# Shifting attention rows to ScalarE, doubling the last block's side steps and spreading the reload of the node features in a two-layer graph network kernel

## The chip, the core and the metric

The kernel runs on one core of one Trainium2 chip. The metric is the device time of one execution in microseconds (us), as the median of several runs. TensorE is called PE, VectorE DVE, ScalarE ACT, GpSimd POOL and SyncE SP, as in the profile. PE multiplies, DVE and ACT work elementwise, POOL issues the indirect transfers (gathers and scatters of rows), and SP issues the plain transfers.

## What is computed

There are 1250 nodes with 512 features and 40000 edges, sorted by destination. The first layer is graph attention with 8 heads, followed by a dense network; the second layer adds up edge messages and ends in two dense layers with batch norm. Cut to what matters here:

```python
# layer 0, h = layer_norm(x)
xl = (h @ Wl).reshape(-1, HEADS, C); xr = (h @ Wr).reshape(-1, HEADS, C)
e = einsum('ehc,hc->eh', leaky_relu(xl[src] + xr[dst], 0.2), att)
ex = exp(e - segment_max(e, dst)[dst])
alpha = ex / (segment_sum(ex, dst)[dst] + 1e-16)
x1 = x + segment_sum(alpha[..., None] * xl[src], dst) + gat_bias
x2 = x1 + gelu(layer_norm(x1) @ W1 + b1) @ W2 + b2
x = layer_norm(x + x2)
# layer 1
msg = relu(x[src] + edge_attr @ W_e + b_e)
h = (1 + eps) * x + segment_sum(msg, dst)
h = silu(bn(h @ W1 + b1)); h = silu(bn(h @ W2 + b2))
return layer_norm(x + h)
```

## The kernel before, in words

Nodes are sorted by their number of incoming edges and cut into ten blocks of 128 (block 9 has 98); the table `KB` says how many edges the largest node of each block has (44 in block 0, 25 in block 9). A "row" of a block is one edge of each of its 128 nodes, one per partition, so a row is a gather of 128 table lines.

**The attention part** (`attention`) goes through the blocks from 9 to 0. A block is cut into groups of at most 20 rows and a group into chunks of at most 5 rows; there are 22 groups and 77 chunks. Block 0 has three groups of 20, 16 and 8 rows, with 4, 4 and 2 chunks; they are called A, B and C here, and their chunks A0 to A3, B0 to B3, C0 and C1. In the loop over chunks, `scores` gathers a chunk's rows into `xg` (7 buffers, POOL) and reduces them on DVE to one score per edge and head. At the last chunk of a group follow `softmax` (DVE) and `exp` (ACT). `weigh` is a generator that runs one group behind: while the chunks of one group are scored, those of the group before are multiplied by their softmax weights `w`. In each of its chunks the first `na` rows are multiplied on ACT, with 8 instructions per row (one per head), and the rest in a single DVE instruction; then PE adds all rows up into `sums`. After a group, `leave` copies `sums` out (ACT, `ab`) and folds them on PE (`pacc`), and `merge` adds them to the block's `acc` on DVE.

Beside this the dense part of finished blocks is done in small steps, written as generators:

- `head_of` takes a finished `acc` through transposes and a layer norm to `hT`; its steps lie between `yield`s and are made by `step_others`, which is called once a chunk, after `scores`, `softmax` and `merge` and before `weigh`. A step that yields "late" is continued at the end of the chunk by `step_lates`.
- `body_of` is the two-layer dense network of a block, as 19 parts (16 products of W1, the gelu one part later, the W2 product three parts later). A call of `part` makes one of them; `weigh` calls it under a quota of 3 a chunk, or 4 when a block stands in `ready`. Only one body is under way at a time (`held["py"]`).
- `end_of` adds the residual, normalizes, writes the block to `xo_t` and scatters it to `xb_t`. `step_pres` makes a step of it at the start of a chunk.

The instructions of PE, ACT, DVE and POOL in this part are kept in the order in which the program makes them. After the last chunk the last group is weighed, and a loop finishes the bodies of blocks 1 and 0.

**The edge part** (`second`) starts when all blocks stand in `xb_t`. For each pair of rows two gathers fetch `xs` (12 buffers of two rows), PE makes the edge product `pe`, and DVE adds and accumulates relu (L1871, L1872); every fourth full pair is added on PE and put through relu on ACT (L1867, L1868), and DVE only accumulates it (L1876). Blocks go in the order 9, 0, 1, ..., 8. When a block is complete, `finish` adds the block's own features from `x_out` (L1834) and transposes the result; the first dense layer then runs between later pairs. `x_out` holds all ten blocks; it is loaded from `xo_t` by ten transfers of 256 KB issued by SP at the second pair (`i == 1`), after that pair's add (L1877 to L1880). It is read by `finish` and at the very end.

Then come the two dense layers' normalizations, the second dense layer and the output scatter.

Of the kernel before, what the change touches and what calls it, by code (L numbers as in the profile page):

```python
# [713 lines left out]
ORDER = range(NB - 1, -1, -1)  # L714
# [3 lines left out]
def parts(k, most):  # L718

    n = -(-k // most)  # L720
    cut = [k * i // n for i in range(n + 1)]
    return [(a, b - a) for a, b in zip(cut, cut[1:])]
# [3 lines left out]
def gnn_kernel(ctx, tc, x, src, dst, edge_attr, ln1_g, ln1_b, Wl, Wr, att, gat_bias,  # L726
# [515 lines left out]
    BLOCKS = (NB - 1, *range(NB - 1))  # L1242
# [3 lines left out]
    def attention(s1, xb_t, xo_t, eb_t, back, lone, follow):  # L1246
# [243 lines left out]
        def step(t):  # L1490
            got = next(t, 0)
            if got == 0:
                others.remove(t)
            elif got == "late":
                lates.append(t)

        def step_pres():

            todo = list(pres)
            pres.clear()  # L1500
            for t in todo:
                step(t)
# [25 lines left out]
        def some(n):  # L1528
            for _ in range(min(n, quota[0])):
                quota[0] -= 1  # L1530
                part()
# [56 lines left out]
        def weigh(g):  # L1588

            w, n = g["w"], g["n"]  # L1590
            g["gd"] = gd = sp.tile([P, HEADS], F32, name="gd")
            V.tensor_reduce(gd, w[:, :n, :].rearrange("p n h -> p h n"), axis=AX.X, op=OP.add)
            g["at"], g["rows"] = [0, 0], [sum((cn + 1 - i) // 2 for _, cn in g["cuts"]) for i in range(2)]
            for c, (c0, cn) in enumerate(g["cuts"]):
                na = 1 if g is groups[-1] else (cn + c % 2) // 2
                rest = leave()
                xv = g["xg"][c][:, na:cn, :].rearrange("p n (h c) -> p n h c", c=CX)[:, :, :, 1:]
                V.tensor_mul(xv, xv, w[:, c0 + na:c0 + cn, :, None].to_broadcast([P, cn - na, HEADS, CH]))
                for j in range(c0, c0 + na):
                    xv = row_of(g, j)  # L1600
                    for h in range(HEADS):
                        A.activation(xv[:, h, :], xv[:, h, :], AF.Copy, scale=w[:, j, h:h + 1])
                    some(1)
                    next(rest, 0)
                some(quota[0])
                for _ in rest:
                    pass
                if not c:
                    g["sums"] = [aq.tile([P, D], F32, name=f"sums{k}") for k in range(2)]
                for j in range(cn):  # L1610
                    add_up(g, c0 + j // 2 if j % 2 else c0 + cn - 1 - j // 2, j % 2)
                yield
            weighed.append(g)
# [62 lines left out]
        groups, weighed, folded = [], [], []  # L1676
        for b in ORDER:
            cuts = {0: [(0, 20), (20, 16), (36, 8)], 1: [(0, 16), (16, 16), (32, 8)]}.get(b) or parts(KB[b], GN)
            for k0, n in cuts:
                groups.append(dict(b=b, k0=k0, n=n, first=(k0 == 0), last=(k0 + n == KB[b]), cuts=parts(n, CN), xg=[]))  # L1680
        groups[0]["cuts"] = [(0, 2)] + [(2 + a, k) for a, k in parts(groups[0]["n"] - 2, CN)]
        blk = dict(b=ORDER[0], nxr=nxr9)
        ahead = weighing = None
        piece = [0]
        for i, g in enumerate(groups):
            if g["first"]:
                if i:
                    blk, ahead = ahead, None
                blk["m"] = low
                if g["b"] == 0:  # L1690
                    drain("acc", 2)
                    held["acc"] += 1
                    blk.update(over)
                    blk["acc"] = bp.tile([P, D], F32, name="acc", bufs=3)
                    nc.sync.dma_start(blk["acc"], oa_t)
            g["blk"] = blk
            g["S"] = sp.tile([P, GN + 1, HEADS], F32, name="S", bufs=2)
            nc_ = len(g["cuts"])
            left = len(groups[i - 1]["cuts"]) if i else 0
            for c in range(nc_):  # L1700
                step_pres()
                scores(g, c)
                if c == nc_ - 1:
                    softmax(g)
                if c == 0:
                    if not i:
                        others.append(wr_order())
                    if g["first"] and g["b"] != ORDER[-1]:
                        others.append(slots_of(g["b"] - 1))
                    if g is groups[-1] and held["xx"] < 3:  # L1710
                        rows_of(blk)
                    weighing = weigh(groups[i - 1]) if i else None
                if folded:
                    merge(folded.pop())
                if c == 1 and g["first"] and g["b"] != ORDER[-1]:
                    ahead = normed_of(g["b"] - 1)
                if c == 2 and g["first"] and ahead:
                    others.append(xr_of(ahead))
                if i > 3 and piece[0] < len(pieces):
                    piece_of(piece[0])  # L1720
                    piece[0] += 1
                step_others()
                quota[0] = 4 if ready else 3
                todo = -(-left // (nc_ - c))
                left -= todo
                for _ in range(todo):
                    next(weighing)
                if left == 0 and weighing:
                    next(weighing, 0)
                if not todo:  # L1730
                    for _ in leave():
                        some(1)
                if c == nc_ - 1:
                    exp(g)
                some(quota[0])
                step_lates()
# [34 lines left out]
    def second(s2, early, xb_t, xo_t, eb_t, eps1, back, V, A, T):  # L1771
# [25 lines left out]
        with ExitStack() as s3:  # L1797
# [48 lines left out]
            for i, (n, j, m) in enumerate(pairs):  # L1846
                b, c0, cn = pieces[n]
                if j == 0:
                    if c0 == 0:
                        pd = hq.tile([P, 2, D], F32, name="pd")  # L1850
                        if b == 0:
                            nc.tensor.matmul(pd[:, 0, :], back, h9, start=True, stop=True)
                            nc.vector.memset(pd[:, 1, :], 0.0)
                        else:
                            (nc.vector if n else V).memset(pd, 0.0)
                    if n + 1 < len(pieces):
                        eaTs[n + 1] = turn(n + 1, nc.scalar if n else A)
                at = KO[b] + c0 + j
                xs = xp_.tile([P, 2, D], F32, name="xs")
                for k in range(m):  # L1860
                    gather(xs[:, k, :], xb_t, src_i[:, at + k:at + k + 1])
                if i + 1 < len(pairs):
                    product(i + 1)
                pe, xv, pv = pes.pop(i), xs[:, :m, :], pd[:, :m, :]
                if by_pe(i):
                    for k in range(m):
                        nc.tensor.matmul(pe[:, k, :], ident, xs[:, k, :], start=False, stop=True)  # L1867
                    nc.scalar.activation(xv, pe, AF.Relu)  # L1868
                    late.append((xv, pv))
                else:  # L1870
                    add = nc.vector.tensor_add(xv, xv, pe[:, :m, :])  # L1871
                    nc.vector.scalar_tensor_tensor(pv, xv, 0.0, pv, op0=OP.max, op1=OP.add)  # L1872
                last = c0 + j + m == KB[b]
                if late and (last or not by_pe(i)):
                    xv, pv = late.pop()
                    nc.vector.tensor_add(pv, xv, pv)  # L1876
                if i == 1:  # L1877
                    for k in BLOCKS:
                        after(nc.sync.dma_start(x_out[:, k, :], xo_t[k * P:(k + 1) * P, :]), [add],
                              "behind the first gathers")  # L1880
                if j % 4 or j + m == cn or b > 6:
                    if work is None and todo:
                        work = first_dense(todo.pop(0))
                    if work is not None and next(work, 0) == 0:
                        work = None
                if last:
                    if b == NB - 1:
                        h9 = ep.tile([P, D], F32, name="h9", bufs=1)
                        nc.vector.tensor_copy(h9, pd[:, 0, :])
                        nc.vector.tensor_add(h9, h9, pd[:, 1, :])  # L1890
                    finish(b, pd)
                    todo += ready.get(b, [])
# [125 lines left out]
```

## Time and profile before

| what | value |
|---|---|
| median of 5 runs | 1594.36 us (1588.75 to 1604.56) |
| the profiled execution | 1604.1 us, with a span of 1602.3 us |
| mean granted TensorE clock | 0.871 |
| busy share of the span | PE 76%, DVE 72%, POOL 54%, ACT 45% |
| first to last start of an attention row sum (`sums`) | 124.5 to 858.2 us |
| first to last start of an edge gather (`xs`) | 921.3 to 1455.2 us |
| issue of the ten `x_out` loads | 930.5 to 937.0 us |
| start of the last output scatter | 1597.1 us |

The page lists busy time by engine and line; the view of stretches gives each engine's busy time between two moments, the view of waits says who waited for whom, and the timeline lists one engine's work in order, with the idle time before an item and what ended it in square brackets. Inside the attention part nearly all instructions have the line of one helper (L782), so they are told apart by the tiles that they write and read.

### The profile page before, as it was taken

What the parts mean: (1) busy time and instruction counts of PE and PEld (TensorE: products, weight loads), DVE (VectorE), ACT (ScalarE), POOL (GpSimd) and SP (SyncE); (2) the same over time, 40 slices, a digit from 0 to 9 for tenths busy, and PEclk for the clock granted to TensorE, in tenths of its full rate; (3) what the DMA queues carried; (4) which work ended last, traced back from release to release, by engine and by line L of the source; (5) the groups of instructions that cost most, each with busy time, mean ns of one, the idle gap of its engine ahead of it and who ended that gap; (6) DMA issues with size and microseconds to landing.
All of it is one profiled execution on the core that took longest, in us unless ns stands there. A gap on an engine that the chain in (4) does not pass through costs nothing. (4 is left out here: it accounts for less than half of the span.)

```text
span 1602.3 us, 16505 instructions
## 1 busy us (share of the span) xinstructions
PE 1214.3 (76%) x5204; PEld 572.1 (36%) x5204; DVE 1145.8 (72%) x1472; ACT 716.0 (45%) x2063; POOL 864.0 (54%) x789
## 2 busy tenths in 40 slices
PE   5846669799897969796978945575675988698793
PEld 4431225344353424242534512121221443243552
DVE  6859898888889896979982135676676777668233
ACT  3526467676776757768676201110110221121433
POOL 2368777665767776757530075656465555642002
PEclk8977779999997989898979967888797998899896
DMA  6257966545666665546424185666565565652001
GB/s 204 95 150 217 345 172 174 158 137 163 185 185 181 182 187 158 153 111 167 124 83 139 34 284 159 203 188 190 160 204 171 178 179 180 180 147 75 0 0 67
DMA packets 89152, 251.16 MB, mean 157 GB/s; under 512 B 17214, under 2 KB 19268, under 8 KB 88543
## 3 DMA queue, kind: packets, MB, share of 16 engines
q0 software_dynamic: 61008, 199.11, 43.7%
q1 hardware_dynamic: 28047, 50.91, 9.0%
q8 instruction: 43, 0.70, 0.2%
q14 instruction: 54, 0.44, 0.1%
HBM read 225.86 MB, written 24.22 MB: 156 GB/s over the span
## 5 line engine op out<-in xcount | busy, mean ns | idle before, releaser
L782 POOL DMA_INDIRECT xg<-xl_t,src_i x333 | 422.7, 1269 | 207.6 <-issue 116.7
L749 POOL DMA_INDIRECT xs<-xb_t,src_i x333 | 315.7, 948 | 222.1 <-DVE pd L1872 102.5
L1826 PE MATMUL pe<-we,eaT 64*128 64x512 f32 x666 | 227.3, 742 | 145.5 <-issue 72.4
L782 ACT ACTIVATE xg<-xg,w 128x64 f32<-128x64 f32 x1328 | 331.0, 345 | 0.1
L782 PE MATMUL sums<-xg,ident 64*64 64x512 f32 x1332 | 217.3, 728 | 106.0 <-DVE xg L782 83.6
L1871 DVE TENSOR_TENSOR xs<-xs,pe 128x1024 f32<-128x1024 f32 (+1 forms) x130 | 153.6, 1188 | 124.6 <-remote 77.0
L782 DVE TENSOR_TENSOR z<-xg,nxr 128x1440 f32<-128x1440 f32 (+4 forms) x154 | 197.6, 1324 | 39.6 <-DMA xg<-xl_t,src_i 34.5
L782 DVE TENSOR_REDUCE S<-z 128x32 f32<-128x2080 f32 (+2 forms) x77 | 192.2, 2496 | 2.6
L782 PEld LDWEIGHTS pu<-hT,w 128*128 128x128 f32 x1280 | 163.7, 196 | 69.6 <-issue 61.7
L782 PE MATMUL py<-w,uT 128*128 128x512 f32 x320 | 164.9, 607 | 14.9 <-ACT uT L782 11.5
L782 PE MATMUL pu<-hT,w 128*128 128x128 f32 x1280 | 172.3, 282 | 0.7 <-issue 0.7
L1872 DVE SCALAR_TENSOR_TENSOR pd<-xs,pd 128x1024 f32<-128x1024 f32 (+1 forms) x130 | 155.7, 1197 | 3.3
L1826 PEld LDWEIGHTS pe<-we,eaT 64*128 64x128 f32 x666 | 65.4, 215 | 251.1 <-issue 145.7
L782 PEld LDWEIGHTS sums<-xg,ident 64*64 64x64 f32 x1332 | 60.8, 155 | 252.2 <-issue 117.1
L1868 ACT ACTIVATE xs<-pe 128x1024 f32<-128x1024 f32 x40 | 41.0, 1025 | 220.8 <-PE pe L1867 101.2
L782 DVE TENSOR_TENSOR xg<-xg,w 128x1024 f32<-128x1024 f32 (+2 forms) x77 | 100.1, 1305 | 0.0
L782 ACT ACT_TABLE_LOAD x71 | 91.1, 1283 | 7.3 <-DVE sh L782 4.3
L782 PE MATMUL pacc<-ab,fold 128*64 128x512 f32 x88 | 57.9, 746 | 45.5 <-ACT ab L782 42.8
L1867 PE MATMUL pe<-xs,ident 128*128 128x512 f32 x160 | 89.4, 670 | 0.0
L741 POOL DMA_INDIRECT out_dram<-z,v_i x10 | 10.0, 1004 | 131.9 <-ACT z L782 129.5
L782 DVE TENSOR_TENSOR z<-z,sgn 128x768 f32<-128x768 f32 (+2 forms) x77 | 78.2, 1016 | 0.0
L782 PE MATMUL pz<-z,v 128*128 128x512 f32 (+1 forms) x192 | 71.0, 529 | 6.2 <-ACT z L782 6.2
(264 smaller groups left out, 1298.2 us busy)
## 6 DMA issues: line engine op xcount, KB each, us to landing
eb_t<-fe SPq DMA_DIRECT2D x38, 256.0 KB
ea<-eb_t SPq DMA_DIRECT2D x38, 256.0 KB
w<-in_L_gnn_W_dram SPq DMA_DIRECT2D x8, 1024.0 KB
xg<-xl_t,src_i POOLq DMA_INDIRECT x333
xs<-xb_t,src_i POOLq DMA_INDIRECT x333
v<-in_L_gnn_W_dram SPq DMA_DIRECT2D x2, 2048.0 KB
xo_t<-xo SPq DMA_DIRECT2D x10, 256.0 KB
x_out<-xo_t SPq DMA_DIRECT2D x10, 256.0 KB
```

Of the source, the lines that this page charges most:

```text
L741: s = nc.gpsimd.indirect_dma_start(out=table, out_offset=bass.IndirectOffsetOnAxis(ap=idx, axis=0), in_=rows, in_offset=None, bounds_check ...
L749: return nc.gpsimd.indirect_dma_start(out=rows, out_offset=None, in_=table, in_offset=bass.IndirectOffsetOnAxis(ap=idx, axis=0))
L782: ins = getattr(engine, name)(*args, **kw)
L1826: nc.tensor.matmul(pe[:, k, :], eaTs[n][r, j // 2, :], we[r, :], start=True, stop=not by_pe(i))
L1867: nc.tensor.matmul(pe[:, k, :], ident, xs[:, k, :], start=False, stop=True)
L1868: nc.scalar.activation(xv, pe, AF.Relu)
L1871: add = nc.vector.tensor_add(xv, xv, pe[:, :m, :])
L1872: nc.vector.scalar_tensor_tensor(pv, xv, 0.0, pv, op0=OP.max, op1=OP.add)
```

## The change

Three edits:

1. `weigh`: the number of rows that ACT multiplies in a chunk of `cn` rows goes from half of `cn` (rounded down in chunks with an even index, up in odd ones) to half rounded up in even ones and half of `cn + 2`, rounded down, in odd ones. Before, the last group (C) alone had one such row per chunk; now the last two (B and C) have.
2. In the chunks of block 0, `step_others` is called once more, right after `step_pres` and ahead of `scores`.
3. Only the `x_out` loads of blocks 9 and 0 are issued at the second pair. Each following block's load is issued at the second pair of the block before it in the order.

```diff
@@ weigh
-                na = 1 if g is groups[-1] else (cn + c % 2) // 2
+                na = 1 if g in last else (cn + 1 + c % 2) // 2
@@ attention, after the list of groups
+        last = groups[-2:]
@@ attention, loop over chunks
                 step_pres()
+                if g["b"] == ORDER[-1]:
+                    step_others()
                 scores(g, c)
@@ second, loop over pairs
-                if i == 1:
-                    for k in BLOCKS:
+                if c0 == 0 and j == 2:
+                    for k in BLOCKS[:2] if i == 1 else BLOCKS[BLOCKS.index(b) + 1:BLOCKS.index(b) + 2]:
                         after(nc.sync.dma_start(x_out[:, k, :], xo_t[k * P:(k + 1) * P, :]), [add],
                               "behind the first gathers")
```

## The prediction

> **What bounds the kernel now.** I read the view of stretches first, then the waits of the attention part, then the timelines of the two places that the edits touch. The middle of the attention part, the end of it, and the edge part's first 50 us, as stretches (busy us and count of PE, PEld, DVE, ACT, POOL; granted clock, DMA share, GB/s):
>
> ```profile
> 120.00:823.00 703.00, 560.42 (x2856) 264.65 (x2858) 611.32 (x672) 483.18 (x1634) 486.72 (x391) 0.89 0.61 175
> 820.00:860.00 40.00, 33.08 (x195) 14.85 (x188) 24.71 (x37) 30.05 (x101) 3.02 (x2) 0.91 0.09 30
> 860.00:884.00 24.00, 22.55 (x117) 14.66 (x118) 4.67 (x10) 12.49 (x25) 0.00 (x0) 1.00 0.65 221
> 921.00:976.00 55.00, 21.33 (x51) 6.49 (x47) 18.11 (x16) 2.89 (x4) 37.07 (x39) 0.62 0.79 248
> ```
>
> In the first, DVE is busy 87%, PE 80%, ACT 69%: DVE leads, but no engine is alone. After 820 DVE is no longer it; PE and ACT share the end of the attention, and from 860 to 884 PE works nearly without a gap. From 921 to 976 DVE and PE stand idle for two thirds of the time while the DMA engines are at 79%. What DVE waited for in 120 to 823 (total, times, longest):
>
> ```profile
> DVE z L782 <- DMA xg<-xl_t,src_i: 24.9, 10, 5.6
> DVE t L782 <- PE pm L782: 11.1, 2, 5.9
> DVE t L782 <- PE pacc L782: 10.2, 5, 4.6
> DVE gd L782 <- ACT w L782: 7.8, 2, 4.9
> ```
>
> All its waits come to 83 us. Gathers make up some 25; behind most of the others stands ACT, directly or through PE (`pacc` needs ACT's copy of `sums`, `w` is ACT's exp).
>
> **Edit 1 in the middle (groups before B).** Counting the cuts with both formulas, the two leave 29 rows more on ACT (group B has 4 fewer). DVE's price of a row is a difference of forms: 1748 ns for three rows, 1215 for two, 0.53 us. ACT's: a run of 8 instructions takes 2.02 us (merged, at 339.68). So DVE gives up 29 x 0.53 = 15.5 us and ACT takes on 29 x 2.02 = 58.6 us. Neither is all on the path. The bounds are -15.5 us (ACT's rows wholly in its idle time) and +58.6 us (wholly on the path). ACT sits idle for 703 - 483 = 220 us there, mostly waiting for PE's transposes in chunks with a head or a query projection; in those chunks a further row is cover. In chunks with a body it has little: from 724.7 to 748 it runs without a gap and `sums` at 745.93 starts as ACT's rows end. Queued behind a longer ACT run are the exp (its reader `gd` usually has 7 us of scoring before it), the square root of the norms (same) and the copies of `sums`, for which `merge` already waits 21 us. I keep 60% of DVE's gain, as it leads with 87% and not with 100%: -9.3; and 15% of ACT's cost: +8.8. Sum: 0, in -12 to +12.
>
> The Trainium skill weighs against this edit: "ScalarE: Activation LUTs", "Rules for kernel authors", gives multiplication to VectorE rather than ScalarE, for cost per element. The prices above agree (0.53 against 2.02 us). Taken as a rule for the whole time it would make this part +43 us, the difference of the two costs; the trace limits that by ACT's idle time.
>
> **Edits 1 and 2 at the end of the attention.** Here ACT and PE are the path:
>
> ```profile
> 826.25 1.28 ACT L782 ACT_TABLE_LOAD   x1
> ...
> 847.74 1.28 ACT L782 ACT_TABLE_LOAD   x1
> 849.04 0.26 ACT L782 ACTIVATE w<-S 128x72 f32<-128x72 f32 x1
> ```
>
> ```profile
> 824.62 1.12 PE L782 MATMUL py<-b,one 1*128 1x512 f32 x2
> ...
> 862.63 1.16 PE L782 MATMUL pu<-hT,w 128*128 128x128 f32 x8
> ...
> 883.79 1.12 PE L782 MATMUL py<-b,one 1*128 1x512 f32 x2 [0.78 <-DVE xx L782]
> ```
>
> ACT shows no idle time between these table loads, and group C's exp at 849.04 comes 12 us after its scores stood ready (DVE's last subtraction ends at 837.2). In that stretch ACT has 8 rows of group B, 16.2 us; four go, so 8.1 us leave it. DVE takes them for 4 x 0.53 = 2.1 us, and waits 3.4 us at 827.88 and 7 us at 849.33 in this stretch, so this is covered. PE is next: it was busy for 20.5 of the 23 us from 826 to 849, and one of its 7 parts there goes (below), so that of the 8.1 I let 4 come through (0 to 8).
>
> The second step a chunk: head_of(1) starts in A3 in both, since its `acc` is merged there. Step by step, it now is ready in B2 and not in C0: aT and px in B0, add and statistics at the end of B0, root and norm in B1, transposes at the end of B1, hT in B2. The body of block 1 can't use B2, as that of block 2 holds `py` until B3. So it starts in B3 with quota 4, then 3 and 3: 10 parts before the loop ends, where C0 and C1 made 4 + 3 = 7. Three parts leave the stretch from 862.6 to 883.8, in which PE makes one in 1.75 us (874.16 less the row before): 5.3 us. They go to B3, where PE has gaps of 3.0 and 4.6 us before the rows at 809.95 and 819.03. The hT that ACT waited 7.3 us for at 824.73 also comes early; most of that wait is PE's, so I count 2. hT of block 0 is ready 12 us after its merge, at 876; if body 1 ends earlier than that, the head is next, so 8 us is this part's bound. A new wait: the root in B1 and B3 stands ahead of ACT's rows, about 1 us. Sum at the end: -4 - 5.3, and -1 for the hT less the new wait: -10, in -14 to -2.
>
> **Edit 3.** The ten loads are 10 x 256 KB = 2.6 MB, amid POOL's first gathers. Five-us stretches, and DVE's and ACT's rows:
>
> ```profile
> 935.00:940.00 5.00, 2.50 (x4) 0.53 (x4) 0.08 (x1) 1.02 (x1) 3.80 (x4) 0.84 1.01 354
> 940.00:945.00 5.00, 3.27 (x8) 1.19 (x8) 4.43 (x4) 0.00 (x0) 3.81 (x4) 0.50 1.03 377
> 945.00:950.00 5.00, 5.00 (x15) 1.69 (x13) 3.97 (x4) 0.00 (x0) 3.79 (x4) 0.85 1.04 384
> 950.00:955.00 5.00, 0.04 (x1) 0.00 (x0) 0.00 (x0) 0.00 (x0) 3.80 (x4) 0.84 0.88 250
> ```
>
> ```profile
> 930.52 6.81 SPq L1879 DMA_DIRECT2D x_out<-xo_t  x10
> 966.44 1.22 DVE L1871 TENSOR_TENSOR xs<-xs,pe 128x1024 f32<-128x1024 f32 x1 [17.23 <-remote]
> 974.84 1.02 ACT L1868 ACTIVATE xs<-pe 128x1024 f32<-128x1024 f32 x1 [18.59 <-remote]
> 975.89 1.23 DVE L1876 TENSOR_TENSOR pd<-xs,pd 128x1024 f32<-128x1024 f32 x1 [6.97 <-ACT xs L1868]
> ```
>
> The engines are full from 935 to 950, and then the consumers stand still: DVE for 17.2 and 7.0 us, "remote" being a release that the trace can't name, here a landing. The ninth pair's gathers left POOL at 941 and 943 and are used at 966; the first pair's took 5 us. POOL asks for 256 KB each 1.25 us, 209 GB/s, and 250 were moved after 950, so a backlog drains slowly. Eight of ten loads go: 2.1 MB. The low price is their plain DMA time, 2.1 MB at 377 GB/s, 5.6 us; the high one is both gaps, 24.2 us; below nothing is possible, as the eight return one by one in a stream at a DMA share of 0.58 (1000 to 1480), at most like a gather more at POOL's pace, 8 x 1.25 = 10 us. The reader of each load is some 50 us away. SP's queue holds the edge features behind each load, for its pair's add; they are asked for four pieces ahead, so this costs nothing. DVE's later pace (a pair in about 3 us) is not faster than what it lost, so a gap that goes is kept. I take 14 (between the two, nearer the higher end by the gaps being at the crowding itself) less 2 for the return: -12, in -24 to +2.
>
> The same skill has a rule against it: "DMA: Bandwidth & Descriptors", "Rules for kernel authors", tells to issue a DMA early and wait late. By it the old place is right and edit 3 brings 0, for a total of -10. Here the first reader of `x_out` is at 987 and the last at 1483, so early has no use beyond a block.
>
> **Sum.** 0 - 10 - 12 = -22 us against the profiled 1604.1 us, 1582. That execution stood 0.6% over the median of 1594.4; the same ratio (0.9863) gives **1572 us**.
>
> **Rivals.**
> - *The loads were not the cause* (0.18). Gathers at 209 GB/s fill up anyway, and the gap stays; or it is given back by waits of the later stream, where DVE already waits 60 us for landings. Then -10: 1584. For it: the share is 0.77 still at 955 to 960, when the loads are over.
> - *ACT becomes the bound* (0.20). Place: the chunks with a body of the attention's middle, where `sums` waits for ACT's rows, buffers of `xg` come free late and POOL follows. With a share p of ACT's rows on the path, the middle costs 58.6p - 15.5(1 - p); at p = 0.5 it is +21.6 and eats the other 22. At p = 0.6, +29 and +7 in all: 1601; at 0.75, +40: 1612. I put it at 1606. For it: ACT's gapless runs; against: 220 us of idle time.
> - *All comes through* (0.12). Middle -8, end -14, loads -20: -42, 1552.
> - The forecast with its own spread, 1560 to 1584, has 0.50.
>
> **Numbers.** To hold 8 in 10 the range takes in the forecast, both milder cases and a little more at each end, and leaves out most of ACT's: 1550 to 1594. Half a per cent, 8 us, is about what a measurement of this kernel can tell from no change. Faster by more (below 1586): 0.50 + 0.12 + half of the first rival, 0.71. Slower by more (above 1602): 0.6 of ACT's case, 0.12. Within: 0.17.
>
> **What would show it.** Middle: span from the first to the last `sums` near the old one up to group A, DVE's busy time down by 15 us, ACT's up by 58; wrong if DVE's waits for `w`, `pacc` or gathers grow by over 10. End: `py<-b,one` of block 1 before 820, three parts fewer after the last fold, C's exp within 5 us of its scores. Loads: no idle time of DVE over 8 us between 921 and 1000 on the old scale, the first `finish` at least 10 us earlier after the first gather, and the first to last gather shorter by about 12. If the gap is as long with two loads in its place, edit 3's step is wrong.

## The result, and the profile after

The changed kernel takes 1605.71 us (median of 42 runs, 1597.33 to 1617.81). The kernel before, measured beside it, takes 1596.44 (median of 79 runs, 1586.45 to 1612.89). The ratio is 1.0055, with a 95% interval of 1.0043 to 1.0068: some 9 us slower, where 22 us less were forecast. The profiled execution has a span of 1607.1 us and a mean granted clock of 0.874 (before: 1602.3 and 0.871), so 4.8 us of the loss can be seen in it. The trace of one later kernel (edits 1 and 2 without the loads) fell on a disturbed execution and is not used.

I cut both spans at five places: DVE's end of the first chunk's scoring, its end of block 1's last group and of group A, the first edge gather, and the end.

| stage (us) | before | after | difference |
|---|---|---|---|
| start to first chunk scored | 96.7 | 98.3 | +1.6 |
| the middle, to block 1's last group scored | 646.4 | 646.0 | -0.4 |
| group A's scoring | 38.9 | 48.9 | **+10.0** |
| end of A to first edge gather | 139.3 | 135.9 | -3.4 |
| first edge gather to end | 681.0 | 678.0 | -3.0 |

So the place is group A, block 0's first 20 rows. Two stretches of the changed kernel answer to the first and the last of those shown of before (the second is moved by 7.8 us, as the edge part starts later; the columns are the same):

```profile
120.00:823.00 703.00, 560.74 (x2826) 261.80 (x2826) 586.84 (x660) 530.81 (x1833) 471.32 (x387) 0.89 0.59 173
929.00:984.00 55.00, 22.18 (x57) 6.82 (x53) 20.36 (x17) 2.89 (x4) 38.94 (x41) 0.66 0.72 219
```

In the first, DVE does 24 us less and ACT 48 us more than before in the same 703 us. DVE's smaller share isn't a gain: part of it is waiting. In the second, DVE and PE are nearly as idle as before (busy 20 and 22 us, before 18 and 21), though eight of ten loads are gone. DVE's waits in 120 to 825, changed kernel first, then the two rows of before that grew:

```profile
DVE z L782 <- DMA xg<-xl_t,src_i: 34.3, 15, 5.6
DVE rs L782 <- ACT rs L782: 21.6, 7, 13.5
DVE t L782 <- PE pm L782: 14.5, 2, 8.9
DVE order L782 <- ACT xo L782: 7.7, 2, 5.6
```

```profile
DVE rs L782 <- ACT rs L782: 5.2, 3, 2.6
DVE order L782 <- ACT xo L782: 0.7, 1, 0.7
```

`rs` is the reciprocal root in a norm. ACT makes the square root, DVE reads it in a side step. One wait of 13.5 us makes up most of its growth. The waits for gathers grew too, from the 24.9 us that the prediction shows to 34.3, but the middle took no longer for it. The 13.5 us stand in chunk A0. The timeline of DVE there, and ACT's in front of it:

```profile
761.16 0.17 DVE L782 RECIPROCAL rs<-rs 128x1 f32<-128x1 f32 x1 [13.48 <-ACT rs L782]
...
761.57 2.93 DVE L782 TENSOR_TENSOR z<-xg,nxr 128x1800 f32<-128x1800 f32 x2
```

```profile
745.25 9.65 ACT L782 ACTIVATE xg<-xg,w 128x64 f32<-128x64 f32 x40
754.91 1.28 ACT L782 ACT_TABLE_LOAD   x1
756.21 0.26 ACT L782 ACTIVATE w<-S 128x72 f32<-128x72 f32 x1
758.02 1.50 ACT L782 ACTIVATE hT<-pt,cols 128x128 f32<-128x128 f32 x4 [1.55 <-PE pt L782]
759.54 1.28 ACT L782 ACT_TABLE_LOAD   x1
760.84 0.29 ACT L782 ACTIVATE rs<-mv,ln_eps 128x1 f32<-128x1 f32 x1
761.56 0.81 ACT L782 ACTIVATE xo<-xx,rs 128x512 f32<-128x512 f32 x1 [0.43 <-DVE rs L782]
```

Read them together: DVE has nothing to do from 747.7 on, because its next instruction reads a root that ACT makes at 760.84. ACT first works off 40 row multiplications (five rows), an exp, a block's `hT` and two table loads. The root belongs to `end_of` of an earlier block, since `xo` follows on ACT. A0's scoring, which needs none of it, starts only at 761.57, since the added step stands ahead of `scores` in DVE's queue. In the kernel before, that step comes behind the scoring, and ACT's last run is a row shorter (and the one ahead of it too, 16 multiplications where there are now 24):

```profile
738.67 7.75 ACT L782 ACTIVATE xg<-xg,w 128x64 f32<-128x64 f32 x32
...
756.39 0.16 DVE L782 RECIPROCAL rs<-rs 128x1 f32<-128x1 f32 x1 [2.57 <-ACT rs L782]
```

The end of the attention went as forecast in its form. Group C's exp stands 2 us behind its scores (857.70), and from the last row sum to the first edge gather, called the tail below, it is 57.4 us instead of 62.7 (the last row sum of before starts at 858.6, not at 858.2). Body 1 starts in B3:

```profile
828.41 1.12 PE L782 MATMUL py<-b,one 1*128 1x512 f32 x2
```

But an added step stands in front of C0's scoring too:

```profile
839.24 0.69 DVE L782 TENSOR_TENSOR order<-xo,be_b 128x512 f32<-128x512 f32 x1 [7.80 <-ACT xo L782]
```

At the start of the edge part two loads are issued instead of ten, and the gap stays. Stretches of 5 us, then DVE, then ACT:

```profile
943.00:948.00 5.00, 3.83 (x10) 1.36 (x11) 2.45 (x2) 1.02 (x1) 3.78 (x5) 0.85 0.83 277
948.00:953.00 5.00, 3.51 (x14) 1.01 (x11) 4.96 (x5) 0.26 (x1) 3.78 (x5) 1.00 0.81 256
953.00:958.00 5.00, 1.59 (x4) 0.38 (x2) 0.89 (x1) 0.00 (x0) 3.78 (x5) 1.00 0.70 214
958.00:963.00 5.00, 0.84 (x2) 0.51 (x4) 2.08 (x2) 0.00 (x0) 3.79 (x4) 0.52 0.71 192
```

```profile
960.89 1.22 DVE L1874 TENSOR_TENSOR xs<-xs,pe 128x1024 f32<-128x1024 f32 x1 [6.99 <-remote]
...
972.44 1.23 DVE L1879 TENSOR_TENSOR pd<-xs,pd 128x1024 f32<-128x1024 f32 x1 [9.07 <-issue]
...
982.58 1.22 DVE L1874 TENSOR_TENSOR xs<-xs,pe 128x1024 f32<-128x1024 f32 x1 [8.91 <-remote]
```

```profile
971.39 1.02 ACT L1871 ACTIVATE xs<-pe 128x1024 f32<-128x1024 f32 x1 [18.57 <-DMA xs<-xb_t,src_i]
```

The DMA engines are no longer full (0.83 to 0.70 at 277 to 192 GB/s, where they were at 1.0 and 354 to 384), and the landings are late all the same. The first `finish` comes 67.4 us after the first gather, before 65.9.

### The profile page after: what moved, and what is told of

It reads as the page before. It is cut to its first block, busy times and chain, and to the rows that moved or that the text cites. A ratio compares the mean times of both kernels' runs of the same rounds, so it can differ in the third digit from the quotient of the medians.

```text
span 1607.1 us, 16708 instructions
## 1 busy us (share of the span) xinstructions
PE 1224.2 (76%) x5204; PEld 571.6 (36%) x5204; DVE 1133.6 (71%) x1472; ACT 766.0 (48%) x2265; POOL 856.1 (53%) x789
## 5 line engine op out<-in xcount | busy, mean ns | idle before, releaser
L782 POOL DMA_INDIRECT xg<-xl_t,src_i x333 | 416.9, 1252 | 214.9 <-issue 107.6
L782 ACT ACTIVATE xg<-xg,w 128x64 f32<-128x64 f32 x1528 | 380.1, 344 | 0.1
L782 PEld LDWEIGHTS pu<-hT,w 128*128 128x128 f32 x1280 | 163.8, 196 | 66.8 <-issue 58.6
L782 PEld LDWEIGHTS sums<-xg,ident 64*64 64x64 f32 x1332 | 55.6, 152 | 256.3 <-issue 112.7
L1870 PE MATMUL pe<-xs,ident 128*128 128x512 f32 x160 | 93.3, 697 | 0.0
L782 PE MATMUL pacc<-ab,fold 128*64 128x512 f32 x88 | 55.1, 712 | 41.9 <-ACT ab L782 37.0
L782 DVE TENSOR_TENSOR xg<-xg,w 128x1024 f32<-128x1024 f32 (+2 forms) x77 | 86.8, 1132 | 0.0
```

The costliest lines, as they stand in the source:

```text
L782: ins = getattr(engine, name)(*args, **kw)
```

## The experiments

The kernels of a set ran on one chip, beside the kernel before. Five chips were met, one for each set. On three of them the kernel before takes 1481 us, on the two others 1599 and 1607, so only differences within a set are compared. Differences in us are the ratio less one, times the time of before in that set.

### First set (before: 1481.0 us): the three edits alone, and the steps elsewhere

Theory W: the added steps put DVE behind ACT, the rows cost nothing. Theory R: the added rows are on the path through ACT.

**Rows alone:**

```diff
-                na = 1 if g is groups[-1] else (cn + c % 2) // 2
+                na = 1 if g in last else (cn + 1 + c % 2) // 2
```

> Edit 1 alone (ACT's share of the rows, and one row a chunk in groups B and C). Theory W (the steps ahead of the scores put DVE behind ACT; the rows themselves cost nothing in sum): the middle moves by 1 us at most, as between the two traces up to block 1, and the end gains from the four rows that leave ACT in group B: 1590 to 1597 us against 1596.4. Rival R (ACT's added 58.6 us are the bound): the 10 us and more that the attention part lost are here, so 1604 to 1610 us.

1483.76 us, ratio 1.0019 (1.0005 to 1.0033), +2.8 us: between the two theories.

**Double steps alone:**

```diff
                 step_pres()
+                if g["b"] == ORDER[-1]:
+                    step_others()
                 scores(g, c)
```

> Edit 2 alone (step_others once more, ahead of scores, in block 0's chunks). Theory W: DVE waits for ACT's square root in A0 by some 9 us (13.5 less the 2 rows that ACT has fewer here and what DVE is slower) and for ACT's xo in C0 by some 5 to 8, the tail is 5.3 us shorter, so 1600 to 1608 us against 1596.4. Rival R (the rows are the bound, the steps are a gain): 1589 to 1592 us.

1478.68 us, ratio 0.9992 (0.9981 to 1.0004), -1.2 us. The wait that W names is there, 8.9 us, and group A takes 45.4 us (loads alone: 38.6):

```profile
740.29 0.17 DVE L782 RECIPROCAL rs<-rs 128x1 f32<-128x1 f32 x1 [8.86 <-ACT rs L782]
```

But from A's end to the first edge gather it is 131.0 us instead of 139.5, so the time does not show it.

**Loads alone:**

```diff
-                if i == 1:
-                    for k in BLOCKS:
+                if c0 == 0 and j == 2:
+                    for k in BLOCKS[:2] if i == 1 else BLOCKS[BLOCKS.index(b) + 1:BLOCKS.index(b) + 2]:
```

> Edit 3 alone (x_out block by block). By the traces the stretch from the first edge gather to the end lost 3 us of its 681, so 1591 to 1596 us against 1596.4, and the gap of DVE after the eighth pair is as long as before. By the prediction on record, 1584 us.

1481.5 us, ratio 1.0012 (0.9998 to 1.0025), +1.8 us. No gain, but here there was no long gap to begin with: from first gather to first `finish` 42.1 us with ten loads (rows alone) and 38.8 with two. The 3 us are gone by the end: from first gather to the end it is 570.1 and 572.1.

**All three, the second step behind the first:**

```diff
                 step_pres()
-                if g["b"] == ORDER[-1]:
-                    step_others()
                 scores(g, c)
...
                 step_others()
+                if g["b"] == ORDER[-1]:
+                    step_others()
```

> All three edits, but the second step_others of block 0's chunks stands right behind the first, after scores, softmax and merge. Theory W: the waits of 13.5 and 7.8 us ahead of scores go, the 5.3 us of the tail stay: 1585 to 1592 us against 1605.7 of the change. Rival R (the rows are the bound): within 3 us of the change, 1603 to 1608 us.

1487.58 us, ratio 1.0054 (1.0032 to 1.0076), +8.0 us. W falls as stated: with no step ahead of the scores the loss is still there. But the parts do not add up either (+2.8 - 1.2 + 1.8 = +3.4), so R alone isn't it. Where the 8 us lie stays open: the trace, of the fastest of the six runs, takes 817.2 us from the first chunk's scoring to the first edge gather, about as much as with the loads alone (816.4). The change as it is was never timed on a chip of this kind. The trace with the rows alone shows why the place of the step isn't all: DVE, done with A0's scoring at 741.4, waits for the same root behind it.

```profile
748.05 0.17 DVE L782 RECIPROCAL rs<-rs 128x1 f32<-128x1 f32 x1 [6.62 <-ACT rs L782]
```

### Second set (before: 1607.16 us): the whole again, a rival for the gap, two combinations

**The whole change again** (the diff of the change as it is).

> The whole change again, beside its parts on the same chip. The first four runs gave, as differences to the kernel before of 1481 us: rows alone +2.8, double steps alone -1.2, loads alone +1.8, sum +3.4; all three with the second step behind the first: +8. Theory W (the steps ahead of the scores cost where ACT has the added rows): +7 to +12, more than the sum of its parts, and a wait of DVE for ACT's root of over 8 us in chunk A0. Theory S (three parts that add up and do not touch each other): +2 to +5.

1619.69 us, ratio 1.0086 (1.0055 to 1.0116), +13.8 us; A0's wait for the root is 14.4 us, and group A takes 49.8.

**Pads on lines of their own.** The gathers' padded slots all read line `N` of a table; 30 of 128 slots of block 9 are pads. Here slot p reads line `N + p`.

```diff
-    xl_t = dram.tile([N + 1, XW], F32, name="xl_t")
+    xl_t = dram.tile([N + P, XW], F32, name="xl_t")
...
-        engine.tensor_scalar(s_f, s_n, float(-N), None, op0=OP.add)
+        engine.tensor_scalar(s_f, s_n, padn, None, op0=OP.subtract)
...
-            xb_t = fdram.tile([N + 1, D], F32, name="xb_t")
+            xb_t = fdram.tile([N + P, D], F32, name="xb_t")
```

> The kernel before, with one thing changed: the padded slots of the gathers all read one table line so far; here each partition's pad reads a line of its own (128 lines of zeros or of large negatives in place of one). Theory P (the late landings of the first edge gathers come from many packets on one line of memory, as 30 of 128 slots of block 9 are pads): first edge gather to first finish at least 8 us shorter where it took 66 us, at least 3 us shorter where it took 40, and 0.3 to 1.0 per cent faster in all. Theory Q (landings are slow for another reason): within 0.2 per cent of before.

1609.06 us, ratio 1.0015 (0.9983 to 1.0048); first gather to first `finish` 66.0 us, before 65.9. Theory P falls: the pads aren't what makes the landings late.

**Edits 1 and 2 without the loads** (the first two diffs of the first set together).

> Edits 1 and 2 without the loads. Theory W: the two together cost more than the sum of their single prices (+2.8 - 1.2 = +1.6): +6 to +10, since in A0 DVE stands behind ACT's longer run of rows before it may score. Theory S: 0 to +3.

1617.04 us, ratio 1.0043 (1.0007 to 1.0079), +6.9 us. More than the sum of the two (+1.6), as W expects, though the interval reaches down to +1.

**Edit 1 in blocks 9 to 1 only:**

```diff
-                na = 1 if g is groups[-1] else (cn + c % 2) // 2
+                na = 1 if g is groups[-1] else (cn + c % 2 + (g["b"] > 0)) // 2
```

> Edit 1 in the blocks 9 to 1 alone; block 0 keeps its old rows (24 of the added rows stay, and group B gives none up). The last part of the middle (end of block 1's scoring) against before says what the added rows cost there. Forecast on record: 0 in -12 to +12 for the middle, and -4 for group B's four rows, which this kernel does without. Theory R (the added rows are on the path through ACT's runs): at least +2.8, as much as with all of edit 1. Theory W: -3 to +1, as the rows lie in ACT's idle time before block 0.

1617.08 us, ratio 1.0064 (1.0034 to 1.0094), +10.3 us: R's side. But the trace puts most of its loss in one group. To the end of block 1 it takes 649.3 us (before 646.4), then group A takes 47.1 instead of 38.9, though A's own rows are the old ones and no step was added. ACT's run of rows, and what DVE waits for in A0 and in A1:

```profile
742.56 5.85 ACT L782 ACTIVATE xg<-xg,w 128x64 f32<-128x64 f32 x24
...
749.48 9.66 ACT L782 ACTIVATE xg<-xg,w 128x64 f32<-128x64 f32 x40
...
765.08 0.29 ACT L782 ACTIVATE rs<-mv,ln_eps 128x1 f32<-128x1 f32 x1
```

```profile
765.40 0.16 DVE L782 RECIPROCAL rs<-rs 128x1 f32<-128x1 f32 x1 [6.67 <-issue]
...
780.02 0.69 DVE L782 TENSOR_TENSOR acc<-acc,pacc 128x512 f32<-128x512 f32 x1 [5.23 <-PE pu L782]
```

The first wait is 4.1 us longer than before (2.57). The second occurs in no other trace at this length (with the rows alone it is absent), so it is not shown to come from the rows. The 24 and 40 multiplications are three and five rows of one group: the second of block 1, 16 rows in four chunks, which is weighed while only an 8-row group of two chunks is scored. Its rows are packed into half the time, and edit 1 gives ACT 10 of them instead of 8. That made theory G: the loss is ACT's backlog there.

### Third set (before: 1480.95 us): that group alone

**Edit 1 without that group** (`groups[-5]`), **that group alone, and fewer rows there:**

```diff
-                na = 1 if g is groups[-1] else (cn + c % 2) // 2
+                na = 1 if g in groups[-2:] else (cn + (g is not groups[-5]) + c % 2) // 2
```

```diff
-                na = 1 if g is groups[-1] else (cn + c % 2) // 2
+                na = 1 if g is groups[-1] else (cn + (g is groups[-5]) + c % 2) // 2
```

```diff
-                na = 1 if g is groups[-1] else (cn + c % 2) // 2
+                na = 1 if g in (groups[-1], groups[-5]) else (cn + c % 2) // 2
```

> Edit 1 as it is, but the second group of block 1 (16 rows, weighed while only the two chunks of an 8-row group are scored) keeps its old 8 rows on ACT instead of 10. New theory G (the cost of edit 1 sits at one place: ACT's run of that group's rows ends late, and DVE waits in A0 for the root queued behind it, 6.7 us in two traces with the added rows, 2.6 and 1.3 without): A0's wait at most 3 us, group A's scoring 38 to 40 us instead of 42 to 47, and the time lower than with all of edit 1, so within -4 to +3 of before. Theory R (each added row costs its share wherever it is): two rows of 29 change nothing to be measured, +3 to +10 as with edit 1.

1473.64 us, ratio 0.9952 (0.9934 to 0.9969), **-7.1 us**, where all of edit 1 gave +2.8. Group A takes 36.2 us instead of 42.0. Against the traces with the loads alone, whose attention part is that of before, this one gains nothing to the end of block 1 (639.6 us; there 638.2, and 639.2 in the fifth set), 2.4 us in A (there 38.6 and 38.8) and 3.7 from A to the first edge gather (135.8; there 139.5 and 139.4), where four rows of group B are back on DVE (and two of A on ACT). So the gain doesn't show that more rows on ACT pay. ACT's last runs and DVE's wait in A0, which are to be held against the 24 and 40 multiplications and 6.6 us above:

```profile
722.82 3.94 ACT L782 ACTIVATE xg<-xg,w 128x64 f32<-128x64 f32 x16
...
727.84 7.75 ACT L782 ACTIVATE xg<-xg,w 128x64 f32<-128x64 f32 x32
```

```profile
740.49 0.16 DVE L782 RECIPROCAL rs<-rs 128x1 f32<-128x1 f32 x1 [0.24 <-ACT rs L782]
```

> The other half: only that one group gets its two added rows on ACT, all else as before. Theory G: A0's wait for ACT's root grows from about 2 to between 5 and 7 us, group A's scoring by 3 to 8 us, and +3 to +8 in all, though ACT has only 2 rows (4 us of 716) more. Theory R: under +1.

1479.91 us, ratio 0.9995 (0.9982 to 1.0007), -0.7 us; A0's wait 2.3 us. Theory G misses here: two rows alone cost nothing. The trace has ACT's same runs of 24 and 40, but DVE comes to A0's end at 744.5 instead of 741.4 (rows alone) and ACT's root at 746.5 instead of 747.7, so DVE meets it nearly ready:

```profile
746.79 0.16 DVE L782 RECIPROCAL rs<-rs 128x1 f32<-128x1 f32 x1 [2.27 <-ACT rs L782]
```

Theory G2: it is the meeting of the two. The other added rows relieve DVE, which then stands at A0 earlier, while ACT stands there later. That reading rests on this pair of traces.

> That group gets 4 rows on ACT in place of the 8 of before (one a chunk; DVE takes the others at 0.53 us each). Theory G: A0's wait goes (2.6 or 1.3 us before) and the time falls by 0 to 5. Theory R: -1 to +1.

1480.89 us, ratio 1.0001 (0.9985 to 1.0017). The wait is 0.6 us; there was nothing left to win.

**The same, with one row a chunk in group B, and double steps in B and C alone:**

```diff
-                na = 1 if g is groups[-1] else (cn + c % 2) // 2
+                na = 1 if g in (groups[-1], groups[-2], groups[-5]) else (cn + c % 2) // 2
...
+                if g in groups[-2:]:
+                    step_others()
                 scores(g, c)
```

> The same 4 rows there, one row a chunk in group B too (as in edit 1), and the second step a chunk in groups B and C alone, so that no step stands ahead of the scores in A. If the tail's three parts (-5.3 in two traces) come without the waits of A0: body 1 starts in B3 as with edit 2, the tail from the last row sum to the first edge gather is 58 in place of 63 to 64, and the time is 4 to 10 us under before. If steps ahead of the scores cost the same wherever they stand: DVE waits for ACT's output rows in group C (7 us) and the time is within 3 us of before.

1473.16 us, ratio 0.995 (0.9932 to 0.9967), -7.4 us. Tail 57.4 us, end of A to the first edge gather 130.3 (loads alone: 139.5).

### Fourth set (before: 1599.14 us): the whole change with the two places mended

"Rows mended" keeps 8 rows in that group, "steps mended" makes the double step in B and C only. Against the changed kernel:

```diff
-                na = 1 if g in last else (cn + 1 + c % 2) // 2
+                na = 1 if g in last else (cn + (g is not groups[-5]) + c % 2) // 2
```

```diff
-                if g["b"] == ORDER[-1]:
+                if g in last:
                     step_others()
```

The second kernel also takes back the diff of the loads.

> The whole change with two places mended: the second group of block 1 keeps its 8 rows on ACT, and the double step is made in groups B and C alone. Theory G2 (the loss is ACT's backlog at A0, which the added rows build up together and the early step exposes; everything else of edits 1 and 2 brings what was forecast): A0 without a wait for ACT's root over 3 us, scoring of block 0 as short as before or shorter, tail 58, and 8 to 16 us under before. Theory S (parts add up: -7.3 for the rows, -1 to -4 for the steps, 0 to +2 for the loads): -6 to -11. If the loss lies elsewhere (say in the edge part): above -3.

> The same with the ten loads at the second pair as before. The difference to the run before it is the price of edit 3: -12 by the prediction on record (this run slower by 12), -2 to +2 if the loads never were the cause of the late landings, and +3 or more (this run faster) if the loads by blocks return more than they save.

> The whole change with only the steps mended: double steps in groups B and C alone, all added rows left. Theory G2: A0 still waits 5 to 7 us for the root, behind its scores; better than the whole change by 1 to 5 us, and 6 to 10 us worse than with both mended. If the steps were the only fault: as good as with both mended.

> The whole change with only the rows mended: the second group of block 1 keeps 8 rows on ACT, the double step stays in all of block 0. Theory G2: ACT comes to the root about 4 us earlier, so A0's wait in front of the scores shrinks from 13 to 14 us to 8 to 10, as in the run with the steps alone (8.9); better than the whole change by 4 to 8 us, and 3 to 7 us worse than with both mended. If the rows were the only fault: as good as with both mended.

| kernel | us | ratio | A0's wait | group A | end of A to gather |
|---|---|---|---|---|---|
| whole (first result) | 1605.71 | 1.0055 (1.0043 to 1.0068) | 13.5 | 48.9 | 135.9 |
| rows mended | 1608.13 | 1.0059 (1.0036 to 1.0082) | 10.4 | 46.4 | 139.0 |
| steps mended | 1603.44 | 1.0039 (1.0015 to 1.0062) | 6.6 | 41.9 | 136.2 |
| both mended | 1597.42 | 0.9988 (0.9964 to 1.0013) | 0.6 | 36.5 | 137.1 |
| both mended, ten loads | 1592.98 | 0.9977 (0.9951 to 1.0003) | 0.5 | 36.3 | 134.0 |

DVE's line in A0 with the rows mended, the steps mended, and both:

```profile
751.72 0.17 DVE L782 RECIPROCAL rs<-rs 128x1 f32<-128x1 f32 x1 [10.38 <-ACT rs L782]
```

```profile
762.65 0.16 DVE L782 RECIPROCAL rs<-rs 128x1 f32<-128x1 f32 x1 [6.59 <-ACT rs L782]
```

```profile
754.76 0.16 DVE L782 RECIPROCAL rs<-rs 128x1 f32<-128x1 f32 x1 [0.59 <-issue]
```

The four waits are as G2 had them (13 to 14, 8 to 10 with 10.4 just over, 5 to 7, under 3). Group A follows the wait: 36.5 us without, 41.9, 46.4 and 48.9 with 6.6, 10.4 and 13.5 of it. Mending both takes the loss away, mending one doesn't. In time, mending the rows alone gave back nothing that shows against the first result (+9.4 us here, +8.8 there; +13.8 in the second set), so G2's "4 to 8 better" is not shown. With both mended the gain that G2 forecast (8 to 16) isn't there on this chip: -1.9 and -3.7 us, neither to be told from 0. By the expectation of the first of the two, a result above -3 speaks for a loss elsewhere, say in the edge part; the traces show none there (first gather to end 678.1 and 677.6 us, before 681.0 on another chip). From the first chunk's scoring to the first edge gather the two traces are 4.7 and 11.3 us shorter than before's (820.0 and 813.3 against 824.6); why so little of it shows in the times here, and more at 1481, stays open.

### Fifth set (before: 1480.57 us)

**Both mended, ten loads, the double step in B alone** (against the kernel with both mended and ten loads):

```diff
-                if g in last:
+                if g is last[0]:
                     step_others()
```

> Both places mended, the ten loads as before, and the double step in group B alone. Theory G2: the wait for the output rows ahead of group C's scores (7.0 us in the run with the double step in B and C, 0.5 in the kernel before) goes back to under 2, C's scoring is done 4 to 6 us earlier after B's, the tail keeps its 58 to 59 us if body 1 still begins in B3, and the time is 6 to 14 us under before. If the wait hid work that has to be done anyway: as with the double step in both, 3 to 8 under before.

1473.94 us, ratio 0.9955 (0.9936 to 0.9974), -6.7 us. DVE's wait in front of C's scores, with the double step in B and C, and in B alone:

```profile
822.44 0.69 DVE L782 TENSOR_TENSOR order<-xo,be_b 128x512 f32<-128x512 f32 x1 [6.96 <-ACT xo L782]
```

```profile
813.27 0.69 DVE L782 TENSOR_TENSOR order<-xo,be_b 128x512 f32<-128x512 f32 x1 [1.45 <-ACT xo L782]
```

The first trace is of the fourth set's kind of chip, the second of this one. The wait went, and C's scoring took 19.3 us instead of 24.8. But from C's end to the first edge gather it is 76.8 us instead of 72.8, so most of this wait hid work that comes later anyway. At 1481 us the kernel with fewer rows and late steps, which also has the double step in B and C, compares alike (22.2 and 72.8). The wait in C0 is cheap; the one in A0 was not.

**Loads alone again.**

> Edit 3 alone, once more. On the chip where before takes 1481 us it gave +1.8. Where before takes about 1600: -12 by the prediction on record; -3 to +5 if the landings of the first gathers are late with two loads as with ten.

1481.22 us, ratio 1.0007 (0.9992 to 1.0021). The set met a chip of the 1481 us kind, so edit 3 alone was never timed where the gap is. Beside other parts it was, in two pairs: the kernel with edit 3 is slower by 6.9 us in the second set (whole change against edits 1 and 2) and by 1.8 in the fourth (both mended, with and without). The intervals of the two kernels overlap in both pairs, so neither a gain nor a cost is shown.

The best kernels: both mended with ten loads, 0.9977 (0.9951 to 1.0003) at 1599 us, and at 1481 us the fewer rows with the late steps, 0.995, the rows without one group, 0.9952, and the double step in B alone, 0.9955, which can't be told apart.

## Why the prediction was wrong, point by point

- **Edit 1 in the middle, 0 in -12 to +12: right.** The middle, which I end at group A as the prediction's own sign does, took 646.0 us (before 646.4). The same kernel traced again took 652.7, and five more with added rows on chips of this kind 640.1 to 649.3, so one pair of traces says little; at 1481 us the four traces with the rows take 635.8 to 641.5 and the six with the old ones, or nearly, 636.7 to 643.5. Taken to the end of group A, as "groups before B" has it, it is +9.6, still inside. DVE's price of 0.53 us and ACT's 2.02 us a row held: for 25 rows in all, DVE is busy for 12 us less in the whole span, ACT for 50 more. The Trainium skill's rule in "ScalarE: Activation LUTs", "Rules for kernel authors", to give multiplications to VectorE, was weighed there. Against it as a rule for the whole time: in the third set the 24 rows more that ACT makes up to the end of block 1 cost nothing there (639.6 us against 638.2 and 639.2), though each takes ACT four times as long as DVE. That they gain is not shown, as that kernel's -7.1 us also holds the 4 rows of B that went the rule's way.
- **Edits 1 and 2 at the end of the attention, -10 in -14 to -2: wrong, +6.6** (A +10.0, after it -3.4). The step that failed is "A new wait: the root in B1 and B3 stands ahead of ACT's rows, about 1 us". I looked for it in B only, and there it was about as forecast (1.1 us in B1), and I asked what is queued behind the root on ACT. What is queued behind DVE's *reading* of the root is a chunk's scoring, and the doubled step begins in A0, where ACT was just working off the most crowded group. The prediction follows `head_of(1)` from A3 on; the root in A0 is that of an `end_of` already under way. The wait was 13.5 us there, and 7.8 in C0 for `xo`. Of what I did price, the three parts of the tail measured 5.3 us as forecast: 62.7 or 62.8 us from the last row sum to the first edge gather in every trace without the double step, 57.4 to 57.6 with it, but for 59.1 with the rows mended and with the step in B alone. Body 1 came in B3 as worked out, though after 820, since A had lost 10 us by then. With the steps alone, end of A to first gather went to 131.0 us against 139.5 with the loads alone, -8.5; in the whole change -3.4.
- **ACT as the bound**, a rival at 0.20, put at 1606 us: the right engine, and in part the right mechanism ("the chunks with a body", "gapless runs"), but not spread over the middle. That the changed kernel takes 1605.71 is luck: by the rival's own working, 1606 is a loss of some 34 us in the middle less the other 22, and the middle lost none. I had the stretch in hand (ACT without a gap from 724.7 to 748) and averaged over it with 15%. At this one place all of the two added rows comes through: 4 us more of ACT's work became 6.4 us more of DVE's waiting (0.24 to 6.62). Most of the rest is ACT's wait for PE's transposes ahead of `hT` (1.54 us against 0.18) and DVE, which has a row fewer there.
- **Edit 3, -12 in -24 to +2: wrong, no gain.** The step that failed is the one I had named: the gap is as long with two loads in its place. From first gather to the end, the traces with ten loads (before, rows in the middle, both mended) take 676.0 to 681.0 us, and 689.0 with the pads moved; those with loads by blocks (the two of the whole change, and the three with something mended) 677.3 to 683.0: no gain to be seen, and the 3.0 us of the profile pair are within this scatter. At 1481 it is 570.6 with ten (mean of seven traces) and 571.7 by blocks (three). On the slower chips the first `finish` comes 63.0 to 66.0 us after the first gather in the four with ten loads, 66.8 to 67.6 in the five by blocks. That the engines were full while DVE waited told of two things at once, not of a cause. The rival "the loads were not the cause" was right in this part. The skill's rule in "DMA: Bandwidth & Descriptors", "Rules for kernel authors", to issue early and wait late, gave 0 for this edit; the runs agree with the 0.

What makes the landings late in that gap stays open. It is not the ten loads and not the pads; the DMA engines' mean busy share is no longer full (0.70; as a mean over 16 engines it doesn't rule out that one of them lags). The 9 us between the medians and the 4.8 of the profile pair differ by less than the runs of one kernel scatter.

## What to carry to other kernels

When a step is moved ahead of other work of an engine that keeps the program's order, find for each engine what the step reads, at the first place where it now stands, and how long the writer's queue is at that very moment; then ask what stands behind the waiting instruction. A share that is kept for the average of a stage ("15% of ACT's cost comes through") is no price for the one group whose work is packed into half the usual time. And parts need not add up when one makes the reader earlier and the other the writer later: alone, edits 1 and 2 gave +2.8 and -1.2 us, together +6.9 (on another chip, 1 to 13). Time them together before adding up.

## What the runs showed that was not expected

The same kernel takes 1481 us on three chips and 1599 or 1607 on two. The attention part up to the end of block 1 is much the same (rows alone 641.5 us, before 646.4). Nearly all the difference lies in the edge gathers: first to last 424.1 us with the rows alone at 1481, 533.9 in the kernel before. From one of the 333 gathers to the next that is 1.28 us at 1481, hardly more than the 1.25 at which POOL asks for them (the prediction has it), and 1.61 in the kernel before. So at 1481 POOL's issuing all but sets the pace of this stage, and edit 3 had next to nothing to win there. Their first 55 us at 1481, with ten loads (rows alone) and with two (loads alone):

```profile
911.00:966.00 55.00, 37.08 (x105) 13.06 (x103) 37.60 (x35) 6.93 (x10) 41.61 (x44) 0.81 0.83 267
```

```profile
907.70:962.70 55.00, 37.27 (x109) 13.27 (x109) 39.78 (x37) 7.07 (x10) 41.67 (x44) 0.84 0.78 238
```

DVE is busy for 38 and 40 of 55 us there, where it was 18 and 20. The rate is 267 and 238 GB/s, against 248 and 219: ten loads show in the rate on both kinds, and on neither as a gain in the time. The waits that the trace calls "remote" (77 us before `xs` in the kernel before) don't occur at 1481, where the waits of the same instruction are put down to the gathers' landings (26.9 us). A gain that is planned from such a gap holds, at best, for the chips that have it.
